# Due times of their own for 22 instructions in a planned four-layer graph network kernel

## The chip, the cores and the metric

The kernel runs on one core of a Trainium2 chip. The metric is the device time of one execution in microseconds (us); the time before is 2736.38 us, the median of three runs (2735.53 to 2736.8).

## The reference

The input is x, 8 examples of 2048 nodes with 128 features, and one symmetric adjacency matrix adj of 2048 x 2048 for all of them. Four layers follow each other, each on a normalised copy of x:

```
for layer in 0, 1, 2, 3:
    h = max(layernorm(x), 0)
    x = x + gnn(layer, h)
```

In layers 0, 1 and 3, Wh = h W, two numbers s1 and s2 per node come from Wh by the halves of a vector a, and the output row i is the softmax over the neighbours j of leaky_relu(s1[i] + s2[j], 0.2), times Wh. Layer 0 puts an elu on it. Layer 3 first scales h by a weight per node (plus h, plus a bias), normalises Wh once more, adds it back to the output, and puts an elu on that. Layer 2 has four heads of 32 features: softmax over the neighbours of leaky_relu(h h^T, 0.2), times h.

## The kernel before

**Work.** The adjacency matrix is loaded row block by row block (16 of 128 x 2048 int32, 1024 KB each) and turned by VectorE (DVE, L373) into edge, one byte per pair, which stays on chip. A layer of one example is a *unit*, written (example, layer). In a unit of layer 0, 1 or 3 the softmax is factored: exp of a leaky relu of a sum is a maximum of two products. For a *token* (half of the targets, one block of 128 sources; 32 in a unit) DVE makes zg = max(r, cr) x edge (L758, 128 x 1024) in one of three buffers, and TensorE (PE) multiplies it with y (L767, 16 matmuls, 129 columns: 128 features and the denominator). Ahead of its tokens a unit needs: statistics of x (L462, L495) and a power on GpSimd (POOL, L113), h by ScalarE (ACT, L529; in layer 3 also by node, L536), transposes (L560), their copy h_t (L581), the projection by W (L590), and y, cr by exps (L619 to L643). In layer 3 the statistics of y follow (L462, L657 to L659) and y is *weighted* in four groups q0 to q3 (L668). r is s1 along the free axis: for units (0,0), (0,1), (7,3) PE turns it (L690) and ACT copies each half (L699); for others it is turned into rows (L713, L717), written out and read back. After 16 tokens of a half, DVE divides (L799, L800), ACT and DVE do the elu (L806, L830) and the sum goes to x on DVE (L833, L859) or by an accumulating DMA from POOL (L836). Layer 3 has more steps there (L816, L821 to L825).

In layer 2 a *beat* is a head and one block of 128 sources: two score pieces on PE (L1053, 128 x 1024 each), exp on ACT (L1060), mask by edge on DVE (L1066, 128 x 2048), and the product with the values on PE (L1075, mostly for two beats at once). h is kept as a high part (L955, ACT) and a low part (L959, DVE).

**Symmetry test.** The fast path holds only if adj is symmetric. For row j, symmetry(j) walks the columns up to the diagonal in *blocks* (j, k) of up to 512: PE takes edge of row j from the transposed edges of the rows k/128 and on (L387, L391), in a pair of PSUM banks, and ACT squares and sums (L397). There are 40 blocks. The verdict (L412) reads all sums.

**Order.** The whole program is planned before it is emitted. Each step is an operation of class Plan (add, L183) with an engine, an estimated length, a *due* number, the operations that it needs, and the buffers that it takes and frees. The planner advances all engines; among those operations of an engine that can start within 0.148 us of the first, the one with the least due wins (rank, L188; zg gets a bonus of 54.8). Dues are no times: they are ranks, set by tables (TOKENS, BEATS, LEADS) per unit, half and head. What comes out is one fixed order per engine, plan.order, and that is emitted. On the chip each engine goes through its own list in order and waits by semaphores on what its data need, so estimates and needs of the planner have no effect except through the order.

Of the kernel before, what the change touches and what calls it, by code (L numbers as in the profile page):

```python
# [20 lines left out]
P = 128  # L21
# [19 lines left out]
def adj_preln_d4(ctx: ExitStack, tc: tile.TileContext, x, adj, w0, a0, w1, a1, w3, a3,  # L41
# [126 lines left out]
    L3_PLUS, LESS_US = True, 1.9  # L168
    PLUS_US, PLUS_LAG_US, GATHER_US, GATHER_LAG_US = 1.0, 5.5, 2.2, 6.5

    class Plan:


# [7 lines left out]
                          for name, n in slots.items()}  # L181

        def add(self, engine, us, due, emit, needs=(), takes=(), frees=(), lag=None, tiled=False):  # L183
            op = Op(engine, us, due, emit, needs, takes, frees, self.LAG[engine] if lag is None else lag, tiled)
            self.ops.append(op)
            return op
# [56 lines left out]
    def fast(ctx):  # L243
# [12 lines left out]
        add = plan.add  # L256
# [49 lines left out]
        def projections(layer, due, needs):  # L306
# [12 lines left out]
            if layer == 3:  # L319
                needs = [add("DVE", 0.4, due, gains, needs)]  # L320
            first = last = add("PE", 0.5, due, lambda op: nc.tensor.transpose(
                ps[:, op.got["pair"], :P], wide[k], ident), needs, takes=["pair"])

# [24 lines left out]
            def sums(op):  # L348
                nc.tensor.matmul(at(256, 2), lhsT=ones, rhs=sq, start=True, stop=True)
                if layer == 3:  # L350
                    nc.tensor.matmul(at(384, 4), lhsT=ones, rhs=ga, start=True, stop=True)

            last = add("DVE", 0.5, due, weights_t, [last])
            last = add("PE", 0.6, due, lambda op: nc.tensor.matmul(
                at(128, 2), lhsT=w_oi, rhs=a_sb, start=True, stop=True), [last])
# [6 lines left out]
        rows_in, squares, loaded = [], [], []  # L362
# [16 lines left out]
        def symmetry(j):  # L379

            wide = (j + 1) * P
            for k in range(0, wide, 512):
                w, n = min(512, wide - k), len(squares)

                def differences(op, k=k, w=w):
                    pv = ps[:, op.got["pair"], :]
                    nc.tensor.matmul(pv[:, :w], lhsT=minus_8, rhs=edge_8[:, j, k:k + w],  # L387
                                     start=True, stop=False, skip_group_check=True)
                    for i in range(k // P, (k + w) // P):
                        at = i * P - k  # L390
                        nc.tensor.matmul(pv[:, at:at + P], lhsT=edge_8[:, i, j * P:(j + 1) * P],  # L391
                                         rhs=plus_8, start=False, stop=i == (k + w) // P - 1,
                                         skip_group_check=True)

                due = 115.0 + 9.0 * j
                last = add("PE", 0.1 + 0.1 * w / P, due, differences, [rows_in[j], *units[0, 0].v_ready], takes=["pair"])
                squares.append(add("ACT", 0.6, due, lambda op, w=w, n=n, last=last: nc.scalar.activation(  # L397
                    ps[:, last.got["pair"], :w], ps[:, last.got["pair"], :w], AF.Square,
                    accum_out=bad[:, n:n + 1]), [last], frees=[("pair", last)]))
# [761 lines left out]
        def planned():  # L1161
# [8 lines left out]
            for j in range(NB):  # L1170
                symmetry(j)
# [35 lines left out]
        units, projected = {}, {}  # L1207
# [204 lines left out]
```

## Time and profile before

| | |
|---|---|
| median of three runs | 2736.38 us (2735.53 to 2736.8) |
| the profiled execution | 2736.47 us |
| its span in the profile | 2734.7 us |
| PE matmuls busy / weight loads busy | 2624.4 / 2017.2 us |
| DVE, ACT, POOL busy | 2489.3, 1728.7, 284.4 us |
| a token: zg on DVE (L758) | 768 of 1.278 us |
| a token: 16 matmuls (L767) | 12288 matmuls, 1494.5 us in all |
| a mask (L1066) | 512 of 2.286 us |
| an exp (L1060) | 1024 of 1.114 us |
| a row of edges (L373) | 16 of 1.254 us |
| square of a difference block (L397) | 40 of 0.518 us, 48.8 us idle before them |
| mean granted TensorE clock | 0.992 |

Times are from the start of the span. PE is the matmul side of TensorE, PEld its weight loads, which overlap. A timeline line has a start, a duration, engine, line, operation, out<-in with the tile's shape, and how many; in brackets the idle time of the engine ahead of it and the work that ended it. A line by stretch has start and end, length, then busy time of PE, PEld, DVE, ACT and POOL with their instructions, the granted clock, the DMA share and GB/s.

### The profile page before, as it was taken

The page shows a single profiled execution, that of the slowest core. Times are in us where ns is not written, and L with a number is a line of the kernel's source. Part 1 is how long each engine was busy: PE and PEld are TensorE (multiplying, and loading weights), DVE is VectorE, ACT ScalarE, POOL GpSimd, SP SyncE. Part 2 cuts the span into 40 slices and gives each one's busy share as a digit, 9 for nine tenths or more (in the row PEclk, how much of TensorE's full clock was granted, in tenths as well). Part 3 has the DMA queues.
Part 4 walks back from the last instruction along what each step waited for, and adds up shares of the span by engine and source line. Part 5 has one row for each costly group of instructions (what it writes and reads, how often), then busy time and mean ns, then how long its engine had stood idle before and what let it go on. Part 6 is the DMA issues. An engine that isn't in the chain of part 4 may idle for free. (4 is left out here: it accounts for less than half of the span.)

```text
span 2734.7 us, 49017 instructions
## 1 busy us (share of the span) xinstructions
PE 2624.4 (96%) x20104; PEld 2017.2 (74%) x20104; DVE 2489.3 (91%) x3304; ACT 1728.7 (63%) x2777; POOL 284.4 (10%) x143
## 2 busy tenths in 40 slices
PE   7999999999999999999999999999999899999997
PEld 6899877857776877766777767777785378666687
DVE  7867989999989999998999989999999689999987
ACT  3524464667676675666856567675655956787651
POOL 1200000111101111010101011011111101101010
PEclk9999999999999999999999999999999999999999
DMA  8003333252344233433443432424234311623121
GB/s 313 17 9 84 72 63 62 47 101 55 61 121 72 61 82 55 82 74 63 86 78 55 93 55 78 89 49 79 48 75 88 62 39 33 131 55 71 35 46 34
DMA packets 216874, 196.48 MB, mean 72 GB/s; under 512 B 142896, under 2 KB 178176, under 8 KB 210496
## 3 DMA queue, kind: packets, MB, share of 16 engines
q1 hardware_dynamic: 144112, 156.46, 22.1%
q0 software_dynamic: 72112, 36.73, 11.6%
q8 instruction: 160, 2.62, 0.4%
q14 instruction: 74, 0.61, 0.1%
q10 hardware_dynamic: 416, 0.07, 0.0%
HBM read 123.03 MB, written 33.73 MB: 57 GB/s over the span
## 5 line engine op out<-in xcount | busy, mean ns | idle before, releaser
L1060 ACT ACTIVATE z<-ps,shift 128x1024 f32<-128x1024 f32 x1024 | 1122.3, 1114 | 700.0 <-PE ps L1053 697.5
L767 PEld LDWEIGHTS ps<-y,zg 128*128 128x128 f32 x12288 | 1461.8, 192 | 76.6 <-DVE zg L758 25.2
L767 PE MATMUL ps<-y,zg 128*128 128x129 f32 x12288 | 1494.5, 276 | 17.6 <-DVE zg L758 10.2
L1066 DVE SCALAR_TENSOR_TENSOR z<-z,edge 128x2048 f32<-128x2048 f32 x512 | 1169.5, 2286 | 72.0 <-ACT z L1060 69.5
L758 DVE SCALAR_TENSOR_TENSOR zg<-r,cr,edge 128x1024 f32<-128x1024 f32 x768 | 969.7, 1278 | 101.3 <-PE ps L767 87.7
L1053 PE MATMUL ps<-m,s 128*128 128x512 f32 x2048 | 717.1, 436 | 48.0 <-ACT z L1060 44.5
L1053 PEld LDWEIGHTS ps<-m,s 128*128 128x128 f32 x2048 | 314.3, 190 | 323.1 <-ACT z L1060 219.5
L1075 PE MATMUL ps<-z,v 128*32 128x512 f32 x4096 | 503.0, 603 | 1.7 <-DVE z L1066 1.4
L1075 PEld LDWEIGHTS ps<-z,v 128*32 128x32 f32 x4096 | 103.8, 109 | 235.9 <-issue 190.5
L529 ACT ACTIVATE h<-x,nmrx,rstdx 128x128 f32<-128x128 f32 x512 | 210.5, 491 | 33.6 <-DVE nmrx L118 26.5
L113 POOL TENSOR_TENSOR rstdx<-varx,neg_half 128x16 f32<-128x16 f32 x31 | 130.1, 4197 | 570.1 <-DVE varx L108 561.0
L836 POOL DMA_DIRECT2D x<-oa x40 | 35.9, 898 | 880.0 <-DVE oa L800 271.4
L1100 POOL DMA_DIRECT2D x<-o x31 | 66.1, 2132 | 516.8 <-DVE o L1095 506.1
L590 PEld LDWEIGHTS ps<-rhs,h_t 128*128 128x128 f32 x768 | 98.5, 193 | 15.5 <-DVE h_t L581 4.5
L590 PE MATMUL ps<-rhs,h_t 128*128 128x130 f32 x768 | 104.0, 279 | 4.6 <-DVE h_t L581 3.4
L462 DVE BATCH_NORM_STATS2 st<-x 128x6 f32<-128x128 f32 x496 | 106.0, 278 | 1.6 <-DMA x<-oa 1.6
L560 PE MATMUL ps<-ident,h 128*128 128x128 f32 x512 | 79.7, 277 | 3.7 <-ACT z L1060 2.8
L581 ACT COPY h_t<-ps 128x512 f32<-128x512 f32 x92 | 53.4, 582 | 40.2 <-PE ps L560 40.0
L800 DVE TENSOR_TENSOR oa<-ps,rs 128x384 f32<-128x384 f32 x144 | 73.8, 513 | 5.1
L560 PEld LDWEIGHTS ps<-ident,h 128*128 128x128 f32 x512 | 62.2, 142 | 19.9 <-ACT z L1060 6.4
L806 ACT ACTIVATE oe<-oa 128x1024 f32<-128x1024 f32 x32 | 33.9, 1059 | 56.8 <-DVE oa L825 54.4
L628 ACT ACTIVATE y<-ps,y 128x128 f32<-128x128 f32 x240 | 68.6, 369 | 0.0
(129 smaller groups left out, 835.3 us busy)
## 6 DMA issues: line engine op xcount, KB each, us to landing
s<-halves SPq DMA_DIRECT2D x256, 128.0 KB, 2.7
m<-halves SPq DMA_DIRECT2D x64, 512.0 KB, 6.9
r<-row SPq DMA_DIRECT2D x42, 512.0 KB, 3.8
x<-oa POOLq DMA_DIRECT2D x40, 512.0 KB, 5.0
raw<-in_adj_dram SPq DMA_DIRECT2D x16, 1024.0 KB, 17.0
values<-h SPq DMA_DIRECT2D x32, 256.0 KB, 2.4
halves<-hi SPq DMA_DIRECT2D x128, 64.0 KB, 1.7
halves<-lo SPq DMA_DIRECT2D x128, 64.0 KB, 1.7
```

Of the source, the lines that this page charges most:

```text
L113: nc.gpsimd.tensor_tensor(out=rstd, in0=v, in1=neg_half, op=OP.pow)
L462: nc.vector.bn_stats(out=key["st"][:, n, :], in_=rows()[:, n, :])
L529: nc.scalar.activation(self.h[q][:, k, :], X[self.b][:, n, :], AF.Relu, scale=key["rstd"][:, n:n + 1], bias=key["nmr"][:, n:n + 1])
L560: nc.tensor.transpose(pk[:, k, :], self.h[q][:, k, :], ident)
L590: nc.tensor.matmul(pv[:, k, :C + 2], lhsT=self.h_t[q][:, k * P:(k + 1) * P], rhs=rhs, start=True, stop=True)
L758: nc.vector.scalar_tensor_tensor(z, self.r[half], self.cr[:, 0, jb:jb + 1], edge[:, jb, half * HN:(half + 1) * HN], op0=OP.max, op1=OP.mult)
L767: nc.tensor.matmul(ps[:, self.banks(half, place)[i // 3], k * CE:(k + 1) * CE], lhsT=z[:, i * P:(i + 1) * P], rhs=self.y[:, jb, :], start= ...
L800: nc.vector.tensor_mul(key["a"][:, i0:i1, :], pv[:, :, :C], r[:, i0:i1, None].to_broadcast([P, i1 - i0, C]))
L1053: nc.tensor.matmul(ps[:, lo + c, :], lhsT=self.S[h, jb // HB][:, at:at + P], rhs=self.M[h][:, (c2 * 2 + c) * 512:(c2 * 2 + c + 1) * 512], ...
L1060: nc.scalar.activation(self.z[s][:, c2 * HN:(c2 + 1) * HN], ps[:, lo:lo + 2, :].rearrange("p b t -> p (b t)"), AF.Exp, bias=shift)
L1066: nc.vector.scalar_tensor_tensor(self.z[s], self.z[s], 1.0, edge[:, jb, :], op0=OP.mult, op1=OP.mult, accum_out=self.den[:, h, jb:jb + 1])
L1075: nc.tensor.matmul(ps[c * HD:(c + 1) * HD, 0, :], lhsT=self.V[h][:, jb, :], rhs=z[:, c * 512:(c + 1) * 512], start=jb == 0, stop=jb == NB - 1,
```

## The change

22 operations, named by their index in the order in which they were added, get an amount added to their due number; and a difference block's operation now needs all rows up to its own, where it had needed its own.

```
+    SHIFTS = {
+        30: 15.0, 93: 158.9, 113: -50.7, 115: -69.2, 121: 83.4, 131: -98.9, 135: -82.4, 139: -197.1,
+        143: 102.0, 147: -358.4, 151: -347.8, 1041: 215.9, 1099: -157.5, 2060: -98.7, 2063: -123.3,
+        2886: -204.2, 2890: -250.3, 3168: 266.3, 3549: 134.1, 5962: 12.1, 6178: 39.8, 6183: -12.0,
+    }
...
         def add(self, engine, us, due, emit, needs=(), takes=(), frees=(), lag=None, tiled=False):
+            due += SHIFTS.get(len(self.ops), 0.0)
             op = Op(engine, us, due, emit, needs, takes, frees, self.LAG[engine] if lag is None else lag, tiled)
...
-                last = add("PE", 0.1 + 0.1 * w / P, due, differences, [rows_in[j], *units[0, 0].v_ready], takes=["pair"])
+                last = add("PE", 0.1 + 0.1 * w / P, due, differences, [*rows_in[:j + 1], *units[0, 0].v_ready], takes=["pair"])
```

What the indices are:

| index | operation | 
|---|---|
| 30 | DVE's copy h_t of group q2 of unit (0,0): later |
| 93, 121, 143 | difference blocks (2,0), (9,512), (12,1536): later |
| 113, 115, 131, 135, 139, 147, 151 | blocks (8,0), (8,512), (11,0), (11,1024), (12,512), (13,512), (13,1536): earlier |
| 1041 | the mask of unit (0,2), head 1, beat 6: later |
| 1099 | the load of the values of (0,2), head 2: earlier |
| 2060, 2063 | ACT's rows q1 and node scaling q2 of (1,3): earlier |
| 2886, 2890 | PE's tokens 11 and 13 of (2,3): earlier |
| 3168 | ACT's rows q3 of (3,2): later |
| 3549 | the mask of (3,2), head 3, beat 11: later |
| 5962 | the first score piece of (7,2), head 3, beat 2: later |
| 6178 | the weighting q0 of (7,3): later |
| 6183 | the copy of r, half 0, of (7,3): earlier |

No instruction is added or taken away. Of the planned operations 406 of 2413 on PE, 205 of 1648 on ACT, 284 of 1756 on DVE, 2 of 128 on POOL and 11 of 327 on the DMA queue of SyncE (SP) stand at another place in their engine's list than before. The places lie in five stretches: about 20 to 165, 390 to 600, 945 to 1050, 1452 to 1480 and 2550 to 2690 us. Between them the lists are equal. In the first, PE's list has token 0 ahead of the last turn of r, and blocks (8,512), (8,0), (3,0), (4,0), (11,0), (12,512), (13,512), (13,1536) and (11,1024) between tokens 2 and 19, where it had (2,0) to (8,1024). In the last, ACT's list for (7,3) goes q1, r of half 0, q2, q0, r of half 1, q3, where it was q0, q1, q2, r of half 0, r of half 1, q3.

## Prediction

> **What bounds the kernel now.** I read the page's totals first, then its slices, then busy time stretch by stretch, and last the timeline of the places where TensorE stands still. The totals:
>
> ```profile
> span 2734.7 us, 49017 instructions
> PE 2624.4 (96%) x20104; PEld 2017.2 (74%) x20104; DVE 2489.3 (91%) x3304; ACT 1728.7 (63%) x2777; POOL 284.4 (10%) x143
> ```
>
> TensorE (PE) is the bound, and the change adds or removes none of its instructions. So all there is to win is its idle time: 2734.7 - 2624.4 = 110.3 us, 11.1 of it in the first 20 us and 15.7 in the last 35, which nothing here moves. The busy time by stretch says where the rest lies (start and end; length; busy PE, PEld, DVE, ACT, POOL; clock, DMA share, GB/s):
>
> ```profile
> 30.00:40.00 10.00, 8.45 (x62) 7.74 (x62) 7.97 (x11) 2.71 (x10) 0.00 (x0) 0.82 1.01 418
> 80.00:100.00 20.00, 16.13 (x132) 15.46 (x131) 16.04 (x50) 12.51 (x40) 10.72 (x3) 0.91 0.00 1
> 100.00:120.00 20.00, 17.76 (x159) 16.48 (x158) 13.99 (x23) 11.42 (x34) 0.00 (x0) 0.97 0.17 54
> 380.00:520.00 140.00, 139.94 (x1091) 109.31 (x1084) 130.24 (x147) 77.98 (x96) 9.89 (x6) 1.00 0.25 44
> 560.00:600.00 40.00, 35.61 (x237) 19.92 (x230) 38.96 (x58) 25.17 (x25) 6.98 (x2) 1.00 0.62 131
> 2640.00:2660.00 20.00, 16.71 (x149) 16.35 (x148) 12.31 (x34) 9.15 (x24) 3.84 (x1) 1.00 0.09 27
> ```
>
> The reader is to see that 380 to 520 us is full (0.06 us idle), so that a new order gains nothing there, while 30 to 40, 80 to 120 and 2640 to 2660 have holes, and that at 560 to 600 it is VectorE (DVE) that is full. The holes one by one, on PE's timeline (start, duration, then in brackets the idle time before it and what ended that):
>
> ```profile
> 37.40 0.38 PE L387 MATMUL ps<-edge,minus 128*128 128x512 fp8e4 x1 [0.29 <-ACT ps L397]
> 39.13 2.05 PE L767 MATMUL ps<-y,zg 128*128 128x129 f32 x16 [1.14 <-DVE zg L758]
> ...
> 161.24 0.23 PE L412 MATMUL ps<-bad,one 128*1 128x40 f32 x2 [0.84 <-ACT ps L397]
> ...
> 562.44 1.20 PE L1053 MATMUL ps<-m,s 128*128 128x512 f32 x4 [1.09 <-ACT z L1060]
> ...
> 1002.10 1.20 PE L1053 MATMUL ps<-m,s 128*128 128x512 f32 x4 [1.10 <-ACT z L1060]
> 1004.02 2.05 PE L767 MATMUL ps<-y,zg 128*128 128x129 f32 x16 [0.72 <-DVE zg L758]
> ...
> 2659.69 2.02 PE L767 MATMUL ps<-y,zg 128*128 128x129 f32 x16 [3.14 <-DVE rs L799]
> ```
>
> The wait at 39.13 has its cause on DVE's timeline: the third token's zg stood behind a row of the adjacency matrix that had not landed. And the last one has it on ScalarE's (ACT): the copy of r stands behind three groups of weighting.
>
> ```profile
> 36.66 1.23 DVE L373 TENSOR_SCALAR edge<-raw 128x2048 uint8<-128x2048 int32 x1 [1.96 <-DMA raw<-in_adj_dram]
> 37.80 1.28 DVE L758 SCALAR_TENSOR_TENSOR zg<-r,cr,edge 128x1024 f32<-128x1024 f32 x1
> ```
>
> ```profile
> 2651.93 4.72 ACT L668 ACTIVATE y<-y,f 128x128 f32<-128x128 f32 x12 [0.96 <-DVE f L658]
> 2656.56 1.90 ACT L699 COPY r<-ps 128x1024 f32<-128x1024 f32 x2
> ```
>
> **What the Trainium skill says.** "Perfetto Trace Analysis", Identifying the Most-Contended Engine: matmul busy time is no measure of distance from the peak, weight-load busy time is better. Here they are 96% and 74%, so I use PE's busy time only to find its holes. "TensorE: Matmul & The Clock Gate", Architectural detail: VectorE and ScalarE take their instructions strictly in order, TensorE may only pull weight loads forward. The trace agrees: at 2656.56 the r copy came after 4.72 us of weighting, though its input was ready at 2653.0. So a place in a queue is all that a due time can change. Same page, What's actually happening: after an idle window of some 3.4 us the array runs at half clock. The trace shows a slow token earlier than that: after a hole of 2.30 us, with 1.57 of smaller ones just before, the token at 85.07 took 3.52 us where others take 2.00. So holes that are broken up cost less. "DMA: Bandwidth & Descriptors", Where 436 GB/s comes from: loads from HBM are held to 358 to 435 GB/s. The trace has 418 GB/s between 30 and 40 us, so a row of 1024 KB comes every 1.05 MB / 418 GB/s = 2.5 us, and no new order makes it come sooner.
>
> **The change part by part.** The second part (a difference block needs all rows up to its own) alone should move nothing: the rows are converted in their order on one engine, so row j is the last in any case. Its sense is with the first, where blocks of rows 8 to 13 go early. Work is the same on every engine, so each edit costs nothing in itself; I cost positions.
>
> *Start, 11 edits (-1.5).* In the new order zg of token 0 stands ahead of the last two pieces of y, so DVE has the third token's zg ahead of the row that is waited for: the 1.96 us of waiting takes in a 1.28 us zg. PE gets back 0.29 + 1.14 = 1.4 us by 39 us. From then on to 55 us both orders go at DVE's pace, a row and a zg, 1.23 + 1.28 = 2.5 us a token. By 74 us, where DVE starts 8 us of statistics, the new order is one token further (+1.85), three blocks behind (0.77 us by their widths; one 512 wide takes 0.44 us, from 77.23 to 77.67, where the next token starts), and has used 1.43 less idle: 1.85 - 0.77 - 1.43 = -0.35. After these statistics PE is full to token 31 at 112.67, and has one token (1.85) and 0.62 of blocks less to do: ahead by 0.35 + 1.85 + 0.62 = 2.8. Given back: the eight blocks between token 31 and the next half are larger and wait for ACT's squares (+0.4, half of one square and read, 0.58 + 0.19); four blocks, 0.44 + 0.44 + 0.33 + 0.12 = 1.3, now come after 121 us where PE is full (29.16 busy of 30). The verdict no longer stands right behind the last squares, though three blocks in a row do: 0.84 - 0.4 = 0.4 won. Sum -2.8 + 0.4 + 1.3 - 0.4 = -1.5; ends 0 and -2.8 (if what is given back hides).
>
> *Mask of beat 6 and the values' load (heads of example 0; -1.6).* 390 to 500 us: PE is idle 0.06, so 0 to -0.5; I take -0.2. What counts is that scores and masks arrive further ahead at 540: one to two beats' scores more stand ahead of the last tokens of (3,0). DVE has holes of 0.67, 1.12 and 3.52 us from 543 to 555, then is full to 585; one mask of 2.29 us fits in them. What DVE has less to do when it is the bound comes off PE's 6.3 us of small holes. Against it, the row's statistics and the load behind them may be waited for. Ends -0.5 and -2.3; I take -1.4, six tenths of a mask.
>
> *Rows of (1,3) and (3,2), three edits on ACT (-0.9).* Of 1.10 + 0.72 = 1.82 at 1002 to 1004 I take half: the turned rows move behind more scores, and a token still waits for its zg. Each moved group of four activations is 4 x 0.49 us, behind which the exps (1.11) wait; ACT is busy only 28.5 of 40 there. The one queue move elsewhere is on POOL, a plus DMA of (4,0) ahead of a pow: it costs the pow the 0.9 us of one issue at most, under cover of PE's full 40 us. Ends -1.8 and +0.9.
>
> *Tokens 11 and 13 and a mask (2 of PE, 1 of DVE, -0.1)*: 1440 to 1480 has 39.86 of 40. *A score of (7,2) (-0.2)*: one hole of 0.57 at 2572.6 (ends 0, -0.5).
>
> *End, two edits on ACT (-1.5).* Order before: q0, q1, q2, both r copies, q3; after: q1, r of half 0, q2, q0, r of half 1, q3. A group takes 4.72 / 3 = 1.57, a copy 0.95. Token 0 needs r, then zg, and q0. Before: 3 x 1.57 + 0.95 = 5.67, then zg at once, PE starts 2659.69 - 2651.93 = 7.76 after the first group. After: r at 2.5, zg at 3.9; q0 at 3 x 1.57 + 0.95 = 5.66, PE some 0.3 later: 1.8 won, less 0.3 for a factor chain that may be later. What is late next is q0 itself, and then nothing to the end: PE is full (19.61 and 19.48 of 20), so it is carried. Ends -0.6 and -2.4.
>
> Sum: 1.5 + 1.6 + 0.9 + 0.1 + 0.2 + 1.5 = 5.8. The profiled execution took 2736.47 (span 2734.7 and 1.8 around it), which lies 0.09 over the median, so 2736.38 - 5.8 = 2730.6.
>
> **Rivals.** *Given back (about 2733.4).* The middle gains are only positions; between 560 and 600 DVE is full, 38.96 of 40, and the same masks wait there in any order. Then only the start and the end hold: 1.5 + 1.5 = 3.0. For it speaks DVE's 91%; against it that its holes stand right ahead of that stretch.
>
> *All holes close (about 2727.9).* If the start gives 2.4, 540 to 600 2.3, 1000 us 1.8 and the end 2.0: 8.5. For it: each hole has one named cause, and the edit is at that cause.
>
> *Early blocks hold up PE (about 2738).* Blocks of rows 8, 11, 12 and 13 stand between tokens at 38 to 51 us; PE takes them in order. If a row is converted late, the next token waits with it. By my placing, row 8 is done at 37.9 and its block reached at 38.1; row 13 at 50.2, reached at 50.8: slack of 0.2 to 0.8. Seven such blocks, each late by one conversion (1.23), are 8.6 us, less 5.8 is +2.8; as the 1.4 us won at 39 is in part cover, +1.6. It turns the sign once the mean wait passes 5.8 / 7 = 0.8 us.
>
> *It does nothing* is out: the order of four engines differs.
>
> **Chances.** A measurement here can tell about 0.2%, 5.5 us, from no change. My forecast 0.48 (own range 2728.8 to 2732.4), all holes 0.22, given back 0.25, held up 0.05. The bound, 2730.9, lies just past the forecast: 0.6 of its 0.48 and the 0.22 give faster 0.51; same 0.46; slower by 5.5 us needs more than the hold-up as priced, 0.03. Range: 2725.9, where the best ends of all six places meet (2.8 + 2.8 + 1.8 + 0.2 + 0.5 + 2.4 = 10.5), to 2735.3, where the weaker ends leave 1.1.
>
> **What would show it.** Right: no hole over 0.5 us ahead of the third token near 39, and token 31 of the first half 2 to 3 us earlier; fewer waits on exp at 555 to 585; the 3.14 us at 2659 down to about 1.5. Wrong: waits of a difference block on an edge row (L380) at 38 to 51; or an equal sum of PE's idle time from 540 to 600, with DVE still full. The sum of PE's busy time must stay 2624 within the records lost.

## The result, and the profile after

| | before | changed |
|---|---|---|
| median of the runs | 2736.58 us (2733.09 to 2741.91) | 2730.69 us (2728.13 to 2734.78) |
| ratio | | 0.9978, 95% interval 0.9971 to 0.9984 |
| the profiled execution's span | 2734.7 us | 2729.7 us |

The ratio is 6.0 us less, between 4.4 and 7.9. One of the 22 executions of start_30 below took 7837.35 us and is left out of its ratio. In the new source the lines before add are 7 higher and those after it 8 higher than in the kernel before; in the experiments below the shifts stand on one line, and it is 4.

The totals and the stretches of the changed kernel (columns as before: start and end, length, then busy PE, PEld, DVE, ACT and POOL, the granted clock, DMA share, GB/s):

```profile
span 2729.7 us, 49006 instructions
PE 2621.9 (96%) x20104; PEld 2016.2 (74%) x20104; DVE 2488.5 (91%) x3304; ACT 1727.6 (63%) x2777; POOL 286.1 (10%) x143
```

```profile
30.00:40.00 10.00, 8.56 (x78) 7.87 (x77) 9.02 (x14) 3.14 (x9) 0.00 (x0) 1.00 1.01 416
560.00:600.00 40.00, 35.60 (x240) 21.50 (x233) 38.58 (x52) 24.73 (x26) 6.99 (x2) 1.00 0.73 136
2640.00:2660.00 20.00, 17.65 (x155) 17.14 (x154) 14.36 (x34) 11.06 (x30) 3.84 (x1) 1.00 0.09 27
```

The work is the same to the instruction. The idle time of TensorE (PE) is 107.8 us, where it was 110.3, and its busy time is 2.5 us less as well, although nothing was taken out. So a share of the gain is not in the holes. The holes that the prediction named, on PE's timeline of the changed kernel:

```profile
35.60 2.05 PE L775 MATMUL ps<-y,zg 128*128 128x129 f32 x16 [0.18 <-DVE zg L766]
...
158.03 0.38 PE L395 MATMUL ps<-edge,minus 128*128 128x512 fp8e4 x1 [0.40 <-ACT ps L405]
...
562.64 1.20 PE L1061 MATMUL ps<-m,s 128*128 128x512 f32 x4 [1.10 <-ACT z L1068]
...
1001.45 2.05 PE L775 MATMUL ps<-y,zg 128*128 128x129 f32 x16 [0.39 <-DVE zg L766]
...
2649.86 1.96 PE L698 MATMUL ps<-ident,cr 128*128 128x128 f32 x16 [0.87 <-ACT cr L642]
2654.71 2.02 PE L775 MATMUL ps<-y,zg 128*128 128x129 f32 x16 [1.10 <-DVE rs L807]
```

The third token, at 39.13 before, starts at 35.60 after a wait of 0.18; the verdict's row of blocks waits once for a square, as worked out; the wait of 1.10 at 562 is still there; that of 1.10 at 1002 is gone, and the one of 0.72 behind it is 0.39; and 3.14 at the end became 1.10, with a new one of 0.87 just ahead of it.

**Where the time came from.** The 768 tokens run in one fixed order but for the very first, so the start of the k-th token on PE can be compared between two executions: where the difference changes, time was won or lost. Start of a token, changed less before, in us (first line: its start before):

```
token        16     64    144    208    272    336    416    448    592    656    688    736    767
before       71    192    401    643    885   1109   1411   1524   2043   2351   2503   2660   2718
changed   -3.31  -2.07  -2.11  -2.80  -1.20  -1.95  -3.42  -3.95  -3.96  -6.96  -4.22  -4.99  -5.00
```

In five places the order differs: -2.07 up to token 64, -0.7 from 144 to 208, -0.75 from 272 to 336, -0.5 from 416 to 448, -0.8 from 688 to 736. But it also moves where both kernels have the same lists: +1.6 at token 258, -1.4 between 336 and 416, -3.0 between 592 and 656, +2.7 between 656 and 688. Two things make these jumps. One is PE's granted clock. It falls to half for windows of 3.41 us; one of them lies at 818.5 us in the changed kernel, and the two halves of a score there take 1.18 where others take 0.73 (PE's timeline, then the stretch around it):

```profile
817.41 0.73 PE L1061 MATMUL ps<-m,s 128*128 128x512 f32 x2 [0.28 <-ACT z L1068]
818.41 1.18 PE L1061 MATMUL ps<-m,s 128*128 128x512 f32 x2 [0.27 <-ACT z L1068]
```

```profile
800.00:820.00 20.00, 16.64 (x95) 8.96 (x98) 19.47 (x19) 16.07 (x17) 0.67 (x1) 0.96 0.56 119
820.00:840.00 20.00, 19.27 (x139) 12.54 (x132) 18.04 (x17) 10.77 (x11) 2.96 (x2) 0.95 0.75 130
```

The kernel before has clock 1.00 in both stretches; it has such a window at 1228 us instead, where the changed one has none. Ahead of the tail the execution before had 9 of them, the changed one 7. Between 2105 and 2201 us before has three and the changed one two, at 2088 and 2177: these make the -3.0 (improved, below, has none there and -3.9). The other thing is one transfer, an accumulating DMA into oa, that VectorE (DVE) waits for. DVE's timeline, of before and of the changed kernel:

```profile
2359.09 1.23 DVE L823 TENSOR_TENSOR oa<-oa,gamma_sb 128x1024 f32<-128x1024 f32 x1 [0.21 <-DMA oa<-oe]
```

```profile
2354.86 1.23 DVE L831 TENSOR_TENSOR oa<-oa,gamma_sb 128x1024 f32<-128x1024 f32 x1 [2.95 <-DMA oa<-oe]
```

The lists around it are equal, and the wait was 0.34 to 2.34 in the twelve executions below: it differs from one execution to the next.

### The profile page after: what moved, and what is told of

It is laid out like the page before. It is cut to its first block, busy times and chain, and to the rows that moved or that the text cites. A ratio compares the mean times of both kernels' runs of the same rounds, so it can differ in the third digit from the quotient of the medians.

```text
span 2729.7 us, 49006 instructions
## 1 busy us (share of the span) xinstructions
PE 2621.9 (96%) x20104; PEld 2016.2 (74%) x20104; DVE 2488.5 (91%) x3304; ACT 1727.6 (63%) x2777; POOL 286.1 (10%) x143
```

## The experiments

My theory: the change's gains are local holes of PE, each carried to the end because PE is full behind it. Its rivals: the gains are given back; early blocks hold PE up; and, new with the traces, that half clock windows and not the order make the difference. Eleven of the twelve kernels are the changed one with another set of shifts; shifts_only keeps the shifts and leaves out the second part. Each was timed against the kernel before on the same chip, whose median was 2737.4 to 2737.8 us in these. The token table of all of them, as above, less the first profile of before:

```
token            16     64    144    208    272    336    416    448    592    656    688    736    767
needs_only    -0.67  -0.13  -0.15  +2.72  +2.74  +2.77  +1.32  +1.31  +1.32  +4.52  +5.74  +6.15  +7.16
start_blocks  +0.38  +0.86  +0.84  +3.65  +3.64  +3.67  +2.19  +2.18  +2.16  -0.84  +1.30  +1.29  +2.14
start_30      -3.31  -1.27  -1.01  -0.98  -0.97  -0.99  -2.45  -2.47  -2.49  -5.31  -3.91  -3.53  -2.51
start_only    -2.61  -0.55  -0.57  -0.54  -0.55  -0.52  -2.00  -2.03  -2.04  -5.01  -3.07  -3.09  -2.13
m540          -1.41  -1.49  -1.52  -2.16  -2.15  -2.16  -3.62  -3.63  -3.63  -1.89  -0.41  -0.01  +1.00
mid_late      -1.55  -1.59  -1.59  -1.59  -1.59  -2.34  -3.85  -4.37  -3.24  -7.91  -6.81  -6.41  -5.40
m2570         -1.40  -1.46  -1.48  -1.49  -1.50  -1.54  -1.62  -1.65  -1.67  -4.73  -3.29  -1.82  +0.37
end_only      -1.33  -1.61  -1.64  -1.62  +1.62  +3.22  +3.16  +3.14  +4.33  -0.20  +1.92  +0.03  -0.01
no_start      -0.45  -0.73  -0.75  -1.45  -1.45  -2.17  -2.23  -2.77  -2.80  -5.71  -5.57  -6.34  -6.35
shifts_only   -3.51  -1.75  -1.71  -0.78  -0.79  -1.55  -2.07  -2.63  -2.66  -5.29  -4.08  -4.85  -4.86
no_5962       -3.82  -1.84  -1.86  -2.53  -2.54  -3.28  -1.74  -2.28  -2.24  -5.21  -3.26  -4.85  -4.88
improved      -3.15  -1.00  -1.02  -4.45  -2.55  -3.30  -4.77  -5.33  -5.34  -9.21  -7.14  -8.73  -8.76
```

### needs_only: the second part alone

```
+    SHIFTS = {}
```

> Only the second part of the change: no due time is shifted, and a difference block needs all rows up to its own. My theory: nothing moves on any engine, so 2736.4 us within 1 us of the kernel before on the same chip, and every token of TensorE starts within 0.3 us of where it started before, apart from spells at half clock and late DMAs, which differ from one execution to the next. So this run is also the measure of that: what differs here is not the change's. The rival, that the wider wait delays blocks: slower by 1 us or more, with waits of difference blocks on edge rows.

Ratio 0.9999 (0.9988 to 1.0009). The planned lists are those of before on every engine, and no block waits for an edge row. Yet its profiled execution is 7.1 us longer than that of before: 11 windows at half clock ahead of the tail against 9, two of them at 557 and 571 us, where it lost 2.9. My expectation of 0.3 us in the rest held only between such jumps (-0.13 to -0.15 from 192 to 401 us). So the second part does nothing, and a span of one execution tells nothing below some 7 us; the position between two tokens without a jump does.

### shifts_only: the first part alone

```
-                last = add("PE", ..., [*rows_in[:j + 1], *units[0, 0].v_ready], takes=["pair"])
+                last = add("PE", ..., [rows_in[j], *units[0, 0].v_ready], takes=["pair"])
```

> The 22 shifts without the second part (a difference block needs its own row alone). The lists of all engines are then the same as in the changed kernel, so my theory: the same time, 2730.7 us within 2 us, and tokens at 120 to 190 us between 0.5 and 2.1 us ahead of the kernel before, by how the spells at half clock fall. The rival, that the second part carries a share of the gain: more than 1.5 us slower than the changed kernel.

Ratio 0.9979 (0.9973 to 0.9986), 2731.51 us: as the changed kernel. The planned lists of the two are the same. It is also a second look at the new order: token 64 at -1.75, where the first had -2.07.

### start_only, start_30, start_blocks: the start

```
start_only:
+    SHIFTS = {30: 15.0, 93: 158.9, 113: -50.7, 115: -69.2, 121: 83.4, 131: -98.9, 135: -82.4, 139: -197.1,
+              143: 102.0, 147: -358.4, 151: -347.8}
start_30:
+    SHIFTS = {30: 15.0}
start_blocks: the ten others
```

> Only the 11 shifts of the start: the copy h_t and the ten difference blocks. My theory: tokens after 190 us are 1.5 to 2.1 us ahead of the kernel before and it is carried to the end, about 2734.6 us. The rival that it is given back: ahead by 2 to 3 us at 70 us, but by less than 0.5 after 190 us, and 2736.4 us at the end.

> Only the copy h_t of group 2 of unit (0,0) later, so that zg of token 0 goes ahead of the last pieces of y; the difference blocks as before. My theory by the prediction: the waits of 0.29 and 1.14 us ahead of the third token at 39 us go, since VectorE makes its zg while a row of the matrix has not landed; 1 us or more ahead at 68 us and half of that left at 190 us. The rival, that the blocks' places are what counts: nothing is left at 122 us.

> Only the ten shifts of difference blocks, with the copy h_t at its old place. My theory: zg of the third token still stands behind the row that has not landed, so a hole of 0.5 to 1.2 us stays ahead of that token near 39 us, and the start wins less than 0.3 us. The rival that early blocks of rows 8 to 13 hold TensorE up: waits of difference blocks on edge rows between 34 and 52 us, and tokens at 68 us 1 us or more later.

| | ratio (95% interval) | token 64 |
|---|---|---|
| start_only | 0.9989 (0.9982 to 0.9997) | -0.55 |
| start_30 | 0.9993 (0.9985 to 1.0001) | -1.27 |
| start_blocks | 1.0000 (0.9990 to 1.0010) | +0.86 |

At token 64 the old start now has seven executions of its full order (before 0, needs_only -0.13, m540 -1.49, mid_late -1.59, m2570 -1.46, end_only -1.61, no_start -0.73), mean -1.0, and the new start five (start_only -0.55, shifts_only -1.75, changed -2.07, no_5962 -1.84, improved -1.00), mean -1.44. The means differ by 0.4 us, and within each set the times spread over 1.6: the start's share is some 0.4 us with an uncertainty of about that size, not the 1.5 of the prediction. In its one execution the copy h_t alone is about as far ahead as the new start, and the blocks alone win nothing; with a spread of 1.6 this points to the copy and does not prove it. The rival of held up blocks fails: in the changed kernel, start_only and start_blocks no block waits for an edge row between 34 and 52 us. Two expectations failed too. start_only has the time that was expected of it (2734.75 us) but not the lead of 1.5 to 2.1. And in start_blocks no hole is left ahead of the third token. PE in start_blocks:

```profile
30.22 3.81 PE L771 MATMUL ps<-y,zg 128*128 128x129 f32 x16 [0.53 <-DVE zg L762]
38.40 0.38 PE L391 MATMUL ps<-edge,minus 128*128 128x512 fp8e4 x1 [0.40 <-ACT ps L401]
```

DVE waits 1.81 us for the row here, as it waited 1.96 before; but the first two tokens take 3.81 and 2.63 us, where before had 3.38 and 2.00, so PE comes later itself, and what is late on DVE is not late on PE. In m540 and mid_late PE's first tokens are as slow, and the row is waited for by 0.24 and 0.66 us only.

The times say something that the positions do not. Each timed run lists its mean granted clock. Over the 168 executions of the kernel before in these rounds the time falls by 2.0 us for each 0.001 of clock. start_only and start_30 ran at 0.9935 and 0.9939, before on the same chips at 0.9924 and 0.9928: 0.0011 more, give or take 0.0003. That is worth some 2 us by this slope (an estimate), most of the 3.0 and 1.9 that the two won by time. Why the clock was higher is not shown.

### m540: the mask and the values' load

```
+    SHIFTS = {1041: 215.9, 1099: -157.5}
```

> Only two shifts: the mask of unit (0,2), head 1, beat 6, and the load of the values of head 2. My theory by the prediction: 1.6 us ahead from 600 us on, 2734.8 us; the trace of the changed kernel, where tokens went from 2.1 ahead at 450 us to 2.8 ahead at 643 us, says 0.7, so 2735.7 us. The rival that VectorE's bound takes it back: 0 from 600 us on, 2736.4 us.

From token 144 to 208 -0.64, as the changed kernel (-0.69), no_5962 (-0.67) and no_start (-0.70) have it; ratio 0.9989 (0.9979 to 0.9999). So it is 0.7 and not 1.6, and not 0. On the way its tokens swing from 3.4 us ahead of this to 3.9 us behind, as tokens and scores stand in another order on PE there. DVE's timeline of the changed kernel:

```profile
549.92 2.29 DVE L1074 SCALAR_TENSOR_TENSOR z<-z,edge 128x2048 f32<-128x2048 f32 x1 [0.23 <-ACT z L1068]
556.22 2.29 DVE L1074 SCALAR_TENSOR_TENSOR z<-z,edge 128x2048 f32<-128x2048 f32 x1 [2.27 <-ACT z L1068]
560.41 2.29 DVE L1074 SCALAR_TENSOR_TENSOR z<-z,edge 128x2048 f32<-128x2048 f32 x1 [1.10 <-ACT z L1068]
564.56 2.29 DVE L1074 SCALAR_TENSOR_TENSOR z<-z,edge 128x2048 f32<-128x2048 f32 x1 [0.29 <-ACT z L1068]
...
575.55 0.17 DVE L118 SCALAR_TENSOR_TENSOR nmrx<-varx,rstdx 128x16 f32<-128x16 f32 x1 [0.60 <-POOL rstdx L113]
```

Its holes between 543 and 579 were 0.67 + 1.12 + 3.52 + 0.34 + 0.33 + 0.32 + 0.59 = 6.9 us and are 0.23 + 2.27 + 1.10 + 0.29 + 0.60 = 4.5: 2.4 less, so the mask of 2.29 did find room. A hole of 2.27 for an exp stands where 3.52 for hi had been. But PE's idle time from 540 to 600 us went from 6.3 to 5.5 only. Its waits for exps between 555 and 585 are 5.2 us, after 5.4; what is gone is its wait for the low part of h (PE before):

```profile
555.06 1.20 PE L1053 MATMUL ps<-m,s 128*128 128x512 f32 x4 [0.90 <-DVE lo L959]
```

### mid_late: the stretches at 1000 and 1460 us

```
+    SHIFTS = {2060: -98.7, 2063: -123.3, 2886: -204.2, 2890: -250.3, 3168: 266.3, 3549: 134.1}
```

> Only the six shifts of the stretches at 945 to 1050 and 1452 to 1480 us. My theory: the positions are local, so 0.75 us won between token 288 and token 336 and 0.55 between token 416 and token 448, as in the changed kernel, 2735.4 us by these alone. Its start is the old one: if the old start goes with more spells at half clock (8 to 11 windows of 3.4 us in the five executions with it so far, 6 or 7 in the five with the new one), it has 8 or more ahead of the tail. The rival, that the count is chance: 7 or fewer.

From token 272 to 336 -0.75, from 416 to 448 -0.52; the changed kernel, no_start, shifts_only and no_5962 have -0.72 to -0.76 and -0.53 to -0.56. Ratio 0.9992 (0.9986 to 0.9999). The theory of local positions is borne out, to 0.05 us. The second one had been taken for 0.1, as 1440 to 1480 us is 39.86 busy of 40; but PE's timeline of before has steps that are a little longer than elsewhere and are listed with no hole:

```profile
1448.81 0.66 PE L560 MATMUL ps<-ident,h 128*128 128x128 f32 x4
1449.53 2.05 PE L767 MATMUL ps<-y,zg 128*128 128x129 f32 x16
```

```profile
1445.26 0.60 PE L568 MATMUL ps<-ident,h 128*128 128x128 f32 x4
1445.70 1.95 PE L775 MATMUL ps<-y,zg 128*128 128x129 f32 x16
```

The first fence is before, the second the changed kernel: from the transposes to the token 0.72 and 0.44 us. The token has 2.05 where other tokens have 1.95. Together that is 0.38 of the 0.5. Eight windows at half clock: the count that the expectation drew a line at, so it decides nothing.

### end_only, m2570, no_5962: the end

```
end_only:
+    SHIFTS = {6178: 39.8, 6183: -12.0}
m2570:
+    SHIFTS = {5962: 12.1}
no_5962: all 22 but 5962
```

> Only the two shifts of unit (7,3): weighting q0 later, copy of r half 0 earlier. My theory: the 3.14 us that TensorE waits ahead of the first token of (7,3) falls to about 1.5 and is carried to the end, 2734.9 us. The rival that another wait takes its place (y of q0, which is now third): the wait stays over 2.5 us and the time at 2736.4 us.

> Only that score piece later. My theory: 1.1 us lost between token 688 and token 736 of TensorE, 2737.5 us at the end. The prediction took it for 0.2 us won, 2736.2 us.

> All of the change but the shift of one score piece of (7,2), head 3, beat 2. In the changed kernel the two shifts of the end and this one together brought 0.8 us between 2500 and 2660 us, the two shifts of the end alone 1.9. My theory: the score piece costs 1.1 us there, so this kernel is 1.1 us faster than the changed one: 1.9 us won between token 688 and token 736, the wait ahead of the first token of (7,3) about 1.3 us. The rival: the loss at the end has to do with the other shifts, and this one comes out as the changed kernel, 0.8 us won there.

| | ratio (95% interval) | token 688 to 736 | PE idle ahead of the turn of r and ahead of token 736 |
|---|---|---|---|
| before | | 0 | 0.16 + 3.14 |
| end_only | 0.9985 (0.9974 to 0.9997) | -1.89 | 0.15 + 1.26 |
| m2570 | 1.0009 (0.9998 to 1.0020) | +1.47 | 0.86 + 3.34 |
| changed | 0.9978 (0.9971 to 0.9984) | -0.77 | 0.87 + 1.10 |
| no_5962 | 0.9973 (0.9965 to 0.9981) | -1.59 | 0.15 + 1.26 |

ScalarE's (ACT) timeline of end_only shows the sequence that the prediction worked out, 1.55 for a group and 0.9 for a copy from start to start; then PE:

```profile
2653.84 1.65 ACT L672 ACTIVATE y<-y,f 128x128 f32<-128x128 f32 x4 [0.96 <-DVE f L662]
2655.39 0.99 ACT L703 COPY r<-ps 128x1024 f32<-128x1024 f32 x1
2656.28 3.18 ACT L672 ACTIVATE y<-y,f 128x128 f32<-128x128 f32 x8
2659.37 0.99 ACT L703 COPY r<-ps 128x1024 f32<-128x1024 f32 x1
```

```profile
2659.72 5.49 PE L771 MATMUL ps<-y,zg 128*128 128x129 f32 x47 [1.26 <-DVE rs L803]
```

Token 736 starts at 2659.72, 5.88 after the first group (5.96 had been worked out; 7.76 before), when q0 is done at 2659.4. So the mechanism is right, and 1.9 us are in it. And there is more in it than the position. In seven of the eight executions with the old hole of 3.14 us (3.34 in m2570) a half clock window follows right behind it, at 2653 to 2667 us, and from token 736 to 767 they lose 0.85 to 1.0 us on the first profile of before (2.2 in m2570, with two windows). Of the six with the new end none has such a window, and they lose nothing. The first profile of before is the one of the eight without it, so the positions leave this out: some 0.9 us on average.

The shift of the score piece takes 0.8 to 1.1 of the 1.9 away: 1.1 between end_only and the changed kernel, which have no half clock window near 2615 us, and 0.8 between no_5962 and shifts_only, which both have one. m2570 has one as well, worth 0.4 in other kernels with the old order, so that of its +1.47 some 1.1 is the shift. The run times of no_5962 and the changed kernel do not tell the two apart. With the score piece shifted the lists differ up to the end, and the turn of r comes one token later on PE, with a wait of its own. PE of m2570:

```profile
2650.78 1.96 PE L694 MATMUL ps<-ident,cr 128*128 128x128 f32 x16 [0.86 <-ACT cr L638]
2652.58 1.95 PE L771 MATMUL ps<-y,zg 128*128 128x129 f32 x16
2657.87 2.52 PE L771 MATMUL ps<-y,zg 128*128 128x129 f32 x10 [3.34 <-DVE zg L762]
```

Before, two tokens (3.74 us) ran behind the turn while ACT made r; here one does. The holes are 4.20 in place of 3.30. On the way the tokens are 2.1 us ahead (token 704: -5.39 after -3.29 at 688), but scores are behind by as much, and by token 720 it is given back (-3.43); in the changed kernel likewise -4.22, -6.32 and -4.36.

### no_start: all but the start

```
+    SHIFTS = {1041: 215.9, 1099: -157.5, 2060: -98.7, 2063: -123.3, 2886: -204.2, 2890: -250.3,
+              3168: 266.3, 3549: 134.1, 5962: 12.1, 6178: 39.8, 6183: -12.0}
```

> All of the change but the 11 shifts of the start. By TensorE's positions alone the rest is worth 0.7 + 0.75 + 0.55 + 0.8 = 2.8 us, 2733.8 us, against 2730.7 of the changed kernel. If the new start is worth only its 0.6 us of position, it comes out within 1 us of the changed kernel; if the new start also saves some two windows at half clock, 2.5 to 3 us slower than it, with 8 or more windows ahead of the tail.

Ratio 0.9981 (0.9975 to 0.9987), 2732.89 us: within the changed kernel's interval. Positions: -0.70, -0.72, -0.54 and -0.77, as expected. It had 6 windows at half clock, so the old start with few windows exists. Its mean clock was 0.9927, before on its chip 0.9924; shifts_only, with the start, has 0.9931 and 0.9928. So within the whole change the rival that the new start saves windows is not borne out, although the start alone ran at a higher clock. And as no_start wins 5.2 us by time and 2.7 by position, what the positions leave out does not come from the start alone.

### improved: two more shifts, and not the score piece

```
+    SHIFTS = {... all 22 but 5962 ..., 1218: 964.8, 697: -456.2}
```

> The change without the shift of the score piece of (7,2), with two more: token 16 of (1,1) earlier, the first score piece of (0,2), head 3, beat 4, later. My theory: 1.1 us won at the end, as without the score piece, and up to 0.9 us between 460 and 700 us, so 2729 us, 0.6 to 2 us faster than the changed kernel. The rival: VectorE is full from 560 to 600 us, and nothing is won at 700 us over the changed kernel.

Ratio 0.9965 (0.9952 to 0.9978) to the kernel before, 2728.14 us: 9.6 us less (6 to 13). It is the fastest of all; its interval overlaps that of the changed kernel between 0.9971 and 0.9978, so that it is faster than that one is shown by the positions and likely by the times. A part of the 9.6 is the clock: 0.9938, before on its chip 0.9924. From token 144 to 272 it wins 1.53 where the changed kernel wins 0.7 (by no_5962's -0.68, which has no window there), and at the end 1.59. PE idles 2.76 of 40 us between 560 and 600, where the changed kernel idles 4.40, and DVE is full there now:

```profile
560.00:600.00 40.00, 37.24 (x258) 23.05 (x259) 39.83 (x57) 24.81 (x25) 6.99 (x2) 1.00 0.54 99
```

So the rival (DVE full, nothing to win) fails by the position. DVE's idle time did not shrink for it: from 540 to 600 us it is 4.7 us in both kernels, and lies ahead of 560 now. PE's is 4.0 us there, after 5.5.

## Why the prediction was right, and where it was not

The forecast was 2730.6 us and the median is 2730.69. The total is right; its terms are right in part, and the sum is so close by chance.

| place | prediction | position, measured |
|---|---|---|
| second part | 0 | 0 (needs_only, shifts_only) |
| start | -1.5 | -0.4, uncertain by as much |
| 390 to 600 us | -1.6 | -0.7 |
| 1000 us | -0.9 | -0.75 |
| 1460 us | -0.1 | -0.5 |
| score piece | -0.2 | +0.8 to +1.1 |
| end | -1.5 | -1.9 alone |
| sum | -5.8 | -3.2 |
| half clock behind the hole of the end | not considered | -0.9 |
| run times | -5.8 | -6.0 (-7.9 to -4.4) |

(The sum uses -0.8 for score piece and end together, as the changed kernel has it: 0.4 + 0.7 + 0.75 + 0.5 + 0.8 = 3.2.)

*Right.* That what is won in PE's holes is carried to the end: the win between two tokens comes again in every execution with the same order, to 0.1 us, apart from the start and from half clock windows. That the second part moves nothing. The size at 1000 us, where half of 1.82 had been taken without a working: 1.43 of the two holes closed, one of 0.31 opened at 993 us, and 0.75 was won. The end's mechanism, three groups against one and a copy ahead of token 736, to 0.1 us. And that early blocks find their rows converted.

*The bound.* The prediction took PE's idle time for all that there is to win. It did not count half clock windows, which lie in the busy time, and PE's busy sum, which was to stay at 2624, fell by 2.5.

*The start.* The step "PE gets back 0.29 + 1.14 = 1.4 us by 39 us" failed. The hole of 1.14 is an event of that one execution: six others of the same order show 0 to 0.51 there. PE's first and third token in end_only:

```profile
29.93 3.42 PE L771 MATMUL ps<-y,zg 128*128 128x129 f32 x16 [0.77 <-DVE zg L762]
...
37.71 2.05 PE L771 MATMUL ps<-y,zg 128*128 128x129 f32 x16 [0.50 <-DVE zg L762]
```

The first token ran at half clock before, too (3.38 us). What differs is the row that DVE waits for, 1.96 us before and 0.24 to 1.25 in the six, and in four of them a slower first token (3.81). A hole in the first 40 us, where half clock windows and landing rows decide, cannot be taken as a gain.

*390 to 600 us.* The term was mis-sized: six tenths of a mask off PE's holes. DVE's holes shrank by 2.4, a whole mask, and PE got 0.7, three tenths: its waits for exps stayed, and only the wait for the low part went. The direction, and that DVE's bound does not take all back, was right.

*1460 us.* "39.86 of 40" was read as nothing to win. Steps there were up to 0.3 us longer from start to start without a hole in the list; 0.38 of the 0.5 is seen in them.

*Score piece.* One hole of 0.57 had been looked at, and not where the shift moves PE's list to: the turn of r behind one more token of (6,3). The prediction costed a position and did not follow this one to 2650 us.

*The range.* Its weaker ends leave out the +0.9 that the rows of (1,3) and (3,2) had been given; with it they sum to 0.2 and not to 1.1.

*What is left.* The positions explain 3.2 of 6.0 us, and with the half clock windows behind the hole of the end it is 4.1; the interval begins at 4.4. So the rest is some 2 us by the medians, and little is known of it. More half clock windows are no full answer. In one profiled execution of each kernel their count ahead of the tail is 8 to 11 in before, needs_only, start_blocks, m540, m2570, mid_late and end_only, and 5 to 7 in the seven others, and over the fourteen executions spans less their positions rise by 1.4 us a window (correlation about 0.8), near the 1.2 to 1.6 that a single one costs at 818 us here, 1228 before, 1005 and 1589 in end_only. But over all timed runs the mean clock of no_start and shifts_only is higher than that of before on the same chip by 0.0003 and 0.0004 only, give or take 0.0002. At 2.0 us for 0.001 that is 0.6 to 0.7 us (an estimate), no more than the end's 0.9 already holds. The changed kernel's own 16 runs had 0.9934; the executions of before beside them list no clock. The cause of the rest stays open. The wait for the DMA at 2355 us, by its profiles, is none: it was longer after (2.95) than before (0.21).

## What to carry to other kernels

Where one engine is full, compare the start of the same numbered step in both traces: a shift of order then shows to 0.1 us in one execution, when whole spans differ by 7 us. It is taken against one execution, though, and left out nearly half of what the run times show here; so the run times and their clocks are to be read beside it. A gain by reordering is worth its share of holes that come again in each execution; a hole of one profile near the start, or near a clock drop or a landing, is not one. And a moved step has to be followed to the end of all lists that it changes: here one of 22 shifts cost 0.8 to 1.1 us of some 4 that the others had won by position.

## What was not expected of the hardware

TensorE's granted clock fell to half in windows of 3.41 us, up to three in a row, 5 to 11 times ahead of the tail, and 1 to 8 of these behind 125 us, deep inside the kernel. If the traces are cut into stretches of 3.41 us in step with these windows, each of the 58 falls from full speed there came right behind a stretch in which PE was busy for at most 0.66 of the time. No busier stretch, of over 10000 in the fourteen traces, was followed by one; nor were 101 that were as thin. So in these traces a thin stretch came first each time, and did not suffice. In most places it was a row of waits for exps, of 0.74, 0.27 and 0.27 us (567 to 571, 804 to 821, 1212 to 1238, 1581 to 1589 us), elsewhere holes of 1.10 and 0.72 (1005), or a single one of 2.4 (2612 to 2626) or 3.1 (2653 to 2667). No two executions had all their windows at the same places, though ten of the fourteen had one at 2175 to 2183 us. The Trainium skill ("TensorE: Matmul & The Clock Gate", What's actually happening) has windows of 3.4 us that run free of the kernel, which agrees with the length and with the changing places. It names an idle window as what comes before the drop, while here PE was busy for 0.61 of the 3.41 us ahead of the drop at 818.48 us. A window cost 1.2 to 1.6 us at 818, 1005, 1228 and 1589 us, 0.85 to 1.0 behind the hole of 3.14, and 0 to 0.4 at 2615, where a hole of 2.4 stood ahead of it.
